# Messages and first convolution as one two by two by two block product in seven matmuls

## The chip, the core and the metric

The kernel runs on one core of a Trainium2 chip. The metric is the device time of one execution in microseconds (us); lower is better. The core has a matmul engine (TensorE, PE in the profile, with its weight loads as PEld), a vector engine (VectorE, DVE), an engine for activations and copies (ScalarE, ACT), a general one (GpSimd, POOL) and SyncE (SP), whose queue issues most DMAs. SBUF is the working memory, PSUM the banks that matmuls write and add into.

## What is computed

There are 64 graphs of 256 nodes with 256 features, all float32. Layer 0 is a normalised graph convolution with a residual; layer 1 is the large one. The parts that matter here:

```python
h = jnp.maximum(_layernorm(x, axis=-1), 0.0)          # x after layer 0
xc = jnp.transpose(h, (0, 2, 1))
c = relu(_bn(_conv1d(xc, conv1_w, 0), bn1_g, bn1_b, bn1_m, bn1_v))   # 1 tap: a matrix product
c = _bn(_conv1d(c, conv2_w, 8), ...)                  # 17 taps
x_conv = transpose(relu(c + xc))
s = h @ w_se.T + b_se                                 # 3 columns
sq = jnp.sum(s * s, axis=-1)
dist = sq[:, :, None] + sq[:, None, :] - 2.0 * einsum('bnd,bmd->bnm', s, s)
A = jnp.exp(-dist) * adj
msg = relu(h @ w_msg.T + b_msg)                       # messages
x_nmp = einsum('bnm,bmd->bnd', A, msg)
# a GRU cell with input [x_conv, x_nmp] and state h, then a residual
```

So each graph's h (256 x 256) is multiplied by w_msg (256 columns), by w_se (3 columns) and by the first convolution's scaled weights (256 columns). These are the products of this case.

## The kernel before

**Stages.** A first stage goes over the 64 graphs; a second one goes over them again for the gates of the GRU cell. The 17-tap convolution is done on four chunks of 16 graphs through a transform along the nodes: *spectra* (df), products per frequency (y) and an inverse made of adds on DVE and POOL. The first chunk's spectra, products and inverse, and before them the making of the transformed filters (fs), are "items" that are woven into the first stage.

**One turn of the first stage** (the loop over n, L1285 to L1361) works on several graphs at once. In order, on PE: `turn_h(n-2)` transposes h into hT (records ht); `aggregate(n)` and `project(n)` are layer 0's two products (ag, o); `turn_cols(n-4)`, for even n, transposes the small columns (st); `turn_adj(n+1)` transposes the next adjacency (at); `pass_messages(n-5)` multiplies A by the messages (nm); `messages(n-2)` is h times w_msg and w_se (ms); `distance(n-4)`, for even n, is the product for dist (di); `conv1(n-2)` is the first convolution (c). Between them stand calls of `item()`, eight a turn. While filters are made only the two calls `item(True)`, ahead of messages and ahead of conv1, take one.

**Order on the other engines.** All engines run their queues in the order in which the program issues. After each group of matmuls stands `beat(us)`. A beat does the work that has come due: `after(k, go)` puts `go` on the (k+1)th beat that follows, and what comes due on one beat runs in the order in which it was put there. Then `paced.issue` releases a share of the inverse's adds to DVE, POOL and ACT, by the us of the beat and an estimated cost of each operation. So a beat fixes an order, not a time.

**The work around the change.** After `project(n)`: the DVE rows (two of pre and two of x, `rows`, on the second beat, with the store x2d), their moments on the third, POOL's power and product (rs, nmr) on the fifth, ACT's two halves of h on the seventh and eighth. `turn_h` copies its bank to hT on its second beat, by ACT while paced work is left and else by DVE. `aggregate`, `turn_adj` and `pass_messages` copy their banks (aggT, adjT, xnT) with ACT on their second beat; POOL makes adjH from adjT one beat after that. The adjacency exponentials e are ACT's, the product aT is POOL's.

**Messages and conv1.** Each has a PSUM tile of its own (`ms` two banks, `c1` one; five banks of `ps` serve all else), which `own_bank` (L1014) fills with the bias by an ACT copy of 518 or 512 columns. `to_rows` (L1020) adds four matmuls onto it: two row blocks of 128 nodes times two halves of the features. In `messages`, DVE copies the three columns of w_se to `cols` and squares and sums them (`columns`), and ACT makes the messages with one Relu of 512 columns (mso); in `conv1` one ACT Relu of 512 columns makes c1o, which the store h1d takes. Both on the second beat after the matmuls; the next graph's bias copies on the third.

**Buffers.** Tiles of the pool `work` have two buffers unless another number is given: adjH, aggT, xnT and c1o have two, pre two.

Of the kernel before, what the change touches and what calls it, by code (L numbers as in the profile page):

```python
# [11 lines left out]
FP = mybir.dt.float32  # L12
# [173 lines left out]
def gnn_kernel(  # L186
# [11 lines left out]
    P = 128  # L198
# [48 lines left out]
    def after(beats, go):  # L247
        due.append([beats, go])
# [298 lines left out]
    with ExitStack() as one:  # L547
# [25 lines left out]
        nc.gpsimd.memset(mhalf, -0.5)  # L573

        w0T = wts.tile([P, DC, D], FP, tag="w0T", name="w0T")
        w1T = wts.tile([P, DC, D], FP, tag="w1T", name="w1T")

        wmT = wts.tile([P, DC, D + 3], FP, tag="wmT", name="wmT")
        b0B = wts.tile([P, D], FP, tag="b0B", name="b0B")
        b1B = wts.tile([P, 1, D], FP, tag="b1B", name="b1B")  # L580
        bmB = wts.tile([P, 1, D + 3], FP, tag="bmB", name="bmB")
        w2T = [
            taps.tile([P, KW, D], FP, tag=f"w2T{cc}", name=f"w2T_{cc}") for cc in range(DC)
        ]
# [116 lines left out]
        def small_loads():  # L701
            for k, v in enumerate((bn1_g, bn2_g, bn1_b, bn2_b, bn1_m, bn2_m, bn1_v, bn2_v)):
                sp.dma_start(
                    rows[DC * k : DC * (k + 1), :], v.rearrange("(c p) -> c p", p=P)
                )
            sp.dma_start(wsn, w_se)
            sp.dma_start(bmB[:, 0, 0:D], b_msg.partition_broadcast(P))
            sp.dma_start(bmB[:, 0, D : D + 3], b_se.partition_broadcast(P))

        def small_turns():  # L710

# [9 lines left out]
        def small_norms(t):  # L721

            vec.tensor_copy(bn, t[:, :16])
            ve = prep.tile([P, 4], FP, tag="ve", name="ve")
            vec.tensor_scalar(ve, bn[:, 12:16], EPS, None, ALU.add)
            for cc in range(DC):
                vec.tensor_copy(wmT[:, cc, D : D + 3], t[:, 16 + cc * 4 : 16 + cc * 4 + 3])
            rs = prep.tile([P, 4], FP, tag="rs", name="rs")
            pool.tensor_tensor(rs, ve, mhalf[:, :4], ALU.pow)

            def finish():
                vec.tensor_tensor(sc, bn[:, 0:4], rs, ALU.mult)
                ms = prep.tile([P, 4], FP, tag="ms", name="ms")
                vec.tensor_tensor(ms, bn[:, 8:12], sc, ALU.mult)
                vec.tensor_tensor(sh, bn[:, 4:8], ms, ALU.subtract)
                for c in range(DC):
                    vec.tensor_scalar(dg[:, c, :], ident, sh[:, c : c + 1], None, ALU.mult)
            after(2, finish)

        def small_shift():  # L740

            t = bank("t_b1")
            for c in range(DC):
                pe.matmul(t[:, c * P : (c + 1) * P], ones, dg[:, c, :], start=True, stop=True)

            def keep():
                vec.tensor_copy(b1B[:, 0, :], t[:, :D])
            after(0, keep)

        hold, nat = {}, {}  # L750

# [146 lines left out]
        def turn_adj(g, at=(1, 2), by=pool):  # L898
            s = st[g]
            t = bank(f"at_{g}").rearrange("p (c i) -> p c i", c=NB)  # L900
            for jc in range(NB):
                for ic in range(NB):
                    pe.transpose(
                        t[:, jc, ic * P : (ic + 1) * P], s["at"][:, ic, jc * P : (jc + 1) * P], ident
                    )

            def keep():
                s["adjT"] = work.tile([P, NB, N], FP, tag="adjT", name=f"adjT_{g}", bufs=6)
                act.copy(s["adjT"], t)

            def hat():
                s["adjH"] = work.tile([P, NB, N], FP, tag="adjH", name=f"adjH_{g}")
                by.tensor_tensor(s["adjH"], s["adjT"], eye, ALU.add)
            after(at[0], keep)
            if at[1] is None:
                return hat
            after(at[1], hat)

        def aggregate(g):
# [7 lines left out]
                    )  # L927

            def keep():
                s["aggT"] = work.tile([P, DC, N], FP, tag="aggT", name=f"aggT_{g}")  # L930
                act.copy(s["aggT"], t)
            after(1, keep)

        def project(g):
# [9 lines left out]
            def rows():  # L944
                s["x2"] = x2 = work.tile([P, NB, D], FP, tag="x2", name=f"x2_{g}")
                for ib in range(NB):
                    pre = small.tile([P, D], FP, tag="pre", name=f"pre_{g}_{ib}", bufs=2)
                    vec.scalar_tensor_tensor(
                        pre, t[:, ib, :], s["dis"][:, ib : ib + 1], b0B, ALU.mult, ALU.add
                    )  # L950
                    vec.scalar_tensor_tensor(
                        x2[:, ib, :], pre, 0.0, s["xt"][:, ib, :], ALU.max, ALU.add
                    )
# [39 lines left out]
        def turn_h(g, at=1, by=None):  # L993
# [10 lines left out]
            def keep():  # L1004
# [2 lines left out]
                (act.copy if by or any(paced.lines) else vec.tensor_copy)(s["hT"], t)  # L1007
                nc.sync.dma_start(hT_d[g].rearrange("p (c n) -> p c n", c=DC), s["hT"])
            after(at, keep)


        own = {}

        def own_bank(tag, k, bias):  # L1014
            width = bias.shape[2]
            shape = [P, NB, 512] if tag == "ms" else [P, NB, D]
            own[tag] = t = ps_own.tile(shape, FP, tag=tag, name=f"{tag}_{k}")
            act.copy(t[:, :, :width], bias.broadcast_to([P, NB, width]))

        def to_rows(g, tag, wT):  # L1020
            s, t = st[g], own.pop(tag)
            for nb in range(NB):
                for cc in range(DC):
                    pe.matmul(
                        t[:, nb, : wT.shape[2]], s["hT"][:, cc, nb * P : (nb + 1) * P],
                        wT[:, cc, :], start=False, stop=(cc == DC - 1), skip_group_check=True,
                    )
            return t

        def conv1(g):  # L1030
            t = to_rows(g, "c1", w1T)

            def keep():
                h1 = work.tile([P, NB, D], FP, tag="c1", name=f"c1o_{g}")
                act.activation(h1, t, AF.Relu)
                nc.sync.dma_start(h1_d[g].rearrange("p (c d) -> p c d", c=NB), h1)
            after(1, keep)
            if g + 1 < B:
                after(2, lambda: own_bank("c1", g + 1, b1B))

        def messages(g):

            s, t = st[g], to_rows(g, "ms", wmT)

            def columns():

                own = cols.rearrange("p b s (m k w) -> p b (s m) k w", m=2, k=2)[:, :, :, g % 2]
                vec.tensor_copy(
                    own[:, :, :, 0:3],
                    t[:, :, D : D + 3].unsqueeze(2).broadcast_to([P, NB, 4, 3]),  # L1050
                )
                s3 = own[:, :, 0, 0:3]
                sq = small.tile([P, NB, 3], FP, tag="sq", name=f"sq_{g}")
                vec.scalar_tensor_tensor(sq, s3, -0.5, s3, ALU.mult, ALU.mult)
# [2 lines left out]
                vec.tensor_reduce(own[:, :, 2:4, 3], twice, AX.X, ALU.add)  # L1057

            def keep():
                s["msg"] = work.tile([P, NB, D], FP, tag="ms", name=f"mso_{g}", bufs=4)  # L1060
                act.activation(s["msg"], t[:, :, :D], AF.Relu)
            after(1, columns)
            after(1, keep)
            if g + 1 < B:
                after(2, lambda: own_bank("ms", g + 1, bmB))

        def turn_cols(g):

# [43 lines left out]
        def pass_messages(g):  # L1112
# [7 lines left out]
                    )  # L1120

            def keep():
                xn = work.tile([P, DC, N], FP, tag="xnT", name=f"xnT_{g}")
                act.copy(xn, t)
                nc.sync.dma_start(xn_d[g].rearrange("p (c n) -> p c n", c=DC), xn)
                s.clear()
# [18 lines left out]
        act.activation(warm, mhalf[:, 0:1], AF.Relu)  # L1145

        full = eye.rearrange("p c d -> p (c d)")
        own_ms = ps_own.tile([P, NB, 512], FP, tag="ms", name="first_ms")
        own_c1 = ps_own.tile([P, NB, D], FP, tag="c1", name="first_c1")
        for r, t in enumerate((own_ms[:, 0, :], own_ms[:, 1, :], own_c1)):  # L1150
            at = slice(32 * r, 32 * (r + 1))
            pe.matmul(t, ident[at, :], full[at, :], start=True, stop=True)

        def stats(b):

# [9 lines left out]
        def begin():  # L1165
# [42 lines left out]
            aggregate(3)  # L1208
            beat(1.7)
            turn_adj(4)  # L1210
            own_bank("ms", 0, bmB)
            beat(0.4)
            project(2)
            beat(1.7)
# [1 line left out]
            small_shift()  # L1216
            beat(0.4)
            turn_part(w1T, nat_w1, 0, D, "w1", scale=sc[:, 0:DC])
            own_bank("c1", 0, b1B)
            load(3 * G)  # L1220
            project(3)
            beat(1.7)
            messages(0)
            beat(1.7)
            layer0_in(2 * G, range(2))
            conv1(0)
            beat(1.7)
            T(WI, 2)()
            L(WH, 0)()
            turn_h(1, 0, act)  # L1230
# [2 lines left out]
                go()  # L1233
            layer0_in(2 * G, range(2, NR))
            beat(0.4)
            messages(1)
            beat(1.7)
            later.pop(0)[1]()
            later[2].insert(0, T(WI, 4))
            conv1(1)  # L1240
            beat(1.7)
            weights_by[:] = []

        cv.bank, cv.beat = bank, beat
# [40 lines left out]
        for n in range(4, B + 5):  # L1285
# [27 lines left out]
                    after(4, lambda n=n: degrees(n + G))  # L1313
            beat(1.7)
            item()
            if even and n <= B + 2:
                turn_cols(n - 4)
            beat(0.2)
            if n + 1 < B:
                turn_adj(n + 1)  # L1320
            beat(0.4)
# [1 line left out]
            if n >= 5:  # L1323
                pass_messages(n - 5)
            beat(1.7)
            item(True)
            if n <= B + 1:
                messages(n - 2)
            beat(1.7)
            item()  # L1330
            if even and n <= B + 2:
# [4 lines left out]
                project(n)  # L1336
            beat(1.7)
            item(True)
            if n <= B:
                conv1(n - 2)  # L1340
            elif n == B + 2:
                conv1(B - 1)
            beat(1.7)
            item()
            if later:
                for go in later.pop(0):
# [331 lines left out]
```

## Time and profile before

| | |
|---|---|
| median of 3 runs | 2079.58 us (2076.08 to 2081.04) |
| span of the profiled execution | 2074.4 us |
| first stage in the span | until 844 us |
| of it: filters made (fs) | about 140 to 360 us |
| spectra (df) of the first chunk | about 362 to 478 us |
| products (y) of the first chunk | about 475 to 603 us |
| its inverse alone, no items | 603 to 844 us |
| granted TensorE clock, mean | 0.997 |

The profiled execution is one of the program; its span stands 5.2 us below the median of the runs. A record in a timeline has its start, its duration, engine, line, operation, what it writes and reads, and in brackets the idle time ahead of it and what ended that. Helpers issue most operations, so they all have one line (L102), and they are told apart by the names of their tiles. A float32 matmul stands in the records as two, which overlap, so start to start is the better measure of its cost. Groups that work on the two products, with the mean of a record:

| operation | records | mean |
|---|---|---|
| PE ms<-wmT,h2T, 259 columns | 512 | 391 ns |
| PE c<-w1T,h2T, 256 columns | 512 | 383 ns |
| ACT ms<-bmB, 518 columns (median) | 64 | 594 ns |
| ACT c<-b1B, 512 columns (median) | 64 | 590 ns |
| ACT mso<-ms, 512 columns (median) | 64 | 597 ns |
| ACT c1o<-c, 512 columns (median) | 64 | 597 ns |
| DVE cols<-ms, 24 columns (median) | 64 | 182 ns |

### The profile page before, as it was taken

What the parts mean: (1) busy time and instruction counts of PE and PEld (TensorE: products, weight loads), DVE (VectorE), ACT (ScalarE), POOL (GpSimd) and SP (SyncE); (2) the same over time, 40 slices, a digit from 0 to 9 for tenths busy, and PEclk for the clock granted to TensorE, in tenths of its full rate; (3) what the DMA queues carried; (4) which work ended last, traced back from release to release, by engine and by line L of the source; (5) the groups of instructions that cost most, each with busy time, mean ns of one, the idle gap of its engine ahead of it and who ended that gap; (6) DMA issues with size and microseconds to landing.
All of it is one profiled execution on the core that took longest, in us unless ns stands there. A gap on an engine that the chain in (4) does not pass through costs nothing. (4 is left out here: it accounts for less than half of the span.)

```text
span 2074.4 us, 31212 instructions
## 1 busy us (share of the span) xinstructions
PE 2029.9 (98%) x9977; PEld 1728.6 (83%) x9977; DVE 1403.6 (68%) x3172; ACT 999.2 (48%) x2171; POOL 1108.7 (53%) x1326
## 2 busy tenths in 40 slices
PE   7999999999999999999999999999999999999998
PEld 6877777888888787788888888888888888888887
DVE  5656666544688888237889815989924989965444
ACT  5756666665457676522344532234442234443333
POOL 4343333334775665347667527766626767644433
PEclk9999999999999999999999999999999999999999
DMA  8797987656765554656333455533446524322331
GB/s 282 261 259 245 265 257 248 208 178 224 240 206 198 178 178 138 212 178 204 122 117 117 137 176 190 168 101 118 124 152 199 155 92 129 116 87 89 95 96 61
DMA packets 292488, 352.84 MB, mean 170 GB/s; under 512 B 19523, under 2 KB 232150, under 8 KB 291670
## 3 DMA queue, kind: packets, MB, share of 16 engines
q1 hardware_dynamic: 292038, 346.40, 53.1%
q0 software_dynamic: 288, 4.46, 0.6%
q8 instruction: 80, 1.31, 0.3%
q14 instruction: 82, 0.67, 0.1%
HBM read 224.43 MB, written 126.35 MB: 169 GB/s over the span
## 5 line engine op out<-in xcount | busy, mean ns | idle before, releaser
L102 DVE TENSOR_TENSOR Xf<-y,k 128x256 f32<-128x256 f32 x184 | 69.0, 416 | 177.8 <-PE y L102 174.8
L102 DVE SCALAR_TENSOR_TENSOR Xf<-Xf 128x256 f32<-128x256 f32 (+1 forms) x248 | 185.1, 760 | 6.2 <-ACT Xf L102 5.1
L102 PE MATMUL ta<-T,S 128*128 128x256 f32 x768 | 186.6, 379 | 0.0
L102 PE MATMUL y<-wf,Xf 128*128 128x256 f32 x768 | 182.5, 380 | 1.8 <-DVE Xf L102 1.4
L102 POOL TENSOR_TENSOR rz<-u,p 128x256 f32<-128x256 f32 x64 | 47.8, 747 | 244.4 <-ACT u L102 244.4
L102 POOL TENSOR_TENSOR rs<-ve,mhalf 128x2 f32<-128x2 f32 x65 | 52.1, 801 | 220.0 <-DVE nm L102 218.7
L102 ACT ACTIVATE rz<-rz 128x512 f32<-128x512 f32 x128 | 80.3, 627 | 180.8 <-DVE rz L102 180.8
L102 PEld LDWEIGHTS y<-wf,Xf 128*128 128x128 f32 x768 | 143.9, 190 | 24.1 <-DVE Xf L102 2.6
L102 PEld LDWEIGHTS ta<-T,S 128*128 128x128 f32 x768 | 145.9, 190 | 19.8
L102 PE MATMUL n<-wiT,hx 128*128 128x256 f32 x512 | 152.3, 379 | 0.0
L102 POOL TENSOR_TENSOR xs<-Xf 128x256 f32<-128x256 f32 x92 | 69.8, 765 | 136.2 <-PE y L102 72.2
L102 DVE SCALAR_TENSOR_TENSOR h2l<-rz,h2l 128x256 f32<-128x256 f32 x128 | 102.9, 804 | 53.4 <-POOL h2l L102 53.4
L102 POOL TENSOR_TENSOR aT<-e,adjT 128x512 f32<-128x512 f32 x62 | 83.1, 1357 | 95.0 <-ACT e L102 95.0
L102 PE MATMUL ms<-wmT,h2T 128*128 128x259 f32 x512 | 127.2, 391 | 4.4 <-ACT h2T L102 4.4
L102 PE MATMUL n<-whT,hx 128*128 128x256 f32 x512 | 131.4, 379 | 0.0
L102 PE MATMUL n<-wiT,xcT 128*128 128x256 f32 x512 | 131.4, 379 | 0.0
L102 PE MATMUL nm<-aT,mso 128*128 128x256 f32 x512 | 123.3, 385 | 6.1 <-DVE pre L102 3.6
L102 PE MATMUL ag<-adjH,hs 128*128 128x256 f32 x512 | 124.3, 385 | 4.8 <-POOL adjH L102 2.7
L102 POOL TENSOR_TENSOR adjH<-adjT,eye 128x512 f32<-128x512 f32 x63 | 82.2, 1305 | 83.0 <-ACT adjT L102 81.2
L102 PE MATMUL o<-w0T,aggT 128*128 128x256 f32 x512 | 124.0, 385 | 1.4 <-ACT e L102 0.9
L102 PEld LDWEIGHTS ms<-wmT,h2T 128*128 128x128 f32 x512 | 97.8, 194 | 32.1 <-issue 12.9
L102 PE MATMUL c<-w1T,h2T 128*128 128x256 f32 x512 | 123.0, 383 | 0.0
(190 smaller groups left out, 5259.4 us busy)
## 6 DMA issues: line engine op xcount, KB each, us to landing
wf<-wfd SPq DMA_DIRECT2D x284, 256.0 KB
wfd<-fo SPq DMA_DIRECT2D x32, 576.0 KB
x2d<-x SPq DMA_DIRECT2D x64, 256.0 KB
h2d<-h SPq DMA_DIRECT2D x64, 256.0 KB
hTd<-h2T SPq DMA_DIRECT2D x64, 256.0 KB
h1d<-c1o SPq DMA_DIRECT2D x64, 256.0 KB
xnd<-xnT SPq DMA_DIRECT2D x64, 256.0 KB
h1l<-h1d SPq DMA_DIRECT2D x64, 256.0 KB
```

The costliest lines, as they stand in the source:

```text
L102: return self.tc.keep_in_program_order(getattr(self.engine, op)(*args, **kwargs))
```

## The change

hT of a graph is taken as a two by two block matrix (row blocks of nodes by halves of the features: a11, a21, a12, a22), and the weights as another: the columns of the messages with two of w_se (258 columns), beside those of the first convolution with the third of w_se and one column of zeros (258). The product of the two is made with seven block products in place of eight. For that

- four sums of hT's blocks (128 x 128) are made per graph, S0 and S1 by DVE, S3 and S2 by POOL (`h_inputs`, on the beat after hT's copy), and four sums of the weight blocks once (`h_weights`, on POOL);
- the seven matmuls go in two parts: `h_first` (four) where `messages` stood, `h_second` (three) where `conv1` stood. They use three banks, ta, tb and tc, of 258 columns. Three are partial sums that are read and then added to further: ACT copies p1, p5, u2 and p4 to SBUF (258 columns each), and DVE's four adds make the two halves of messages and of the convolution from a copy and a bank each;
- the two bias copies have 258 columns, and the second bias is the difference of the two; Relu is done in place in SBUF, on 512 columns each as before;
- w_se's columns come from two tiles, so DVE copies to `cols` twice, and this happens at the end of a turn, after `h_second`;
- `turn_cols` moves from ahead of `turn_adj` to behind `pass_messages`;
- adjH, aggT, xnT, c1o and pre have one buffer in place of two; the store h1d takes its rows from a tile of 258 columns a row block;
- the last graph's second part comes one turn earlier than its conv1 did, and the beat after `h_second` is 1.3 where that after `conv1` was 1.7.

```diff
@@ constants
-        w1T = wts.tile([P, DC, D], FP, tag="w1T", name="w1T")
-        wmT = wts.tile([P, DC, D + 3], FP, tag="wmT", name="wmT")
+        HC = D + 2
+        wh1 = wts.tile([P, 2, DC, HC], FP, tag="wh1", name="wh1")
+        wmT, w1T = wh1[:, 0], wh1[:, 1]
+        tw = wts.tile([P, 4, HC], FP, tag="tw", name="tw")
...
+        def h_weights():
+            b11, b21, b12, b22 = (wh1[:, w, c] for w in range(2) for c in range(DC))
+            sub(pool, tw[:, 0], b12, b11)
+            sub(pool, tw[:, 1], b22, tw[:, 0])
+            sub(pool, tw[:, 3], b21, tw[:, 1])
+            sub(pool, tw[:, 2], b22, b12)
@@ turn_h
             after(at, keep)
+            after(at + 1, lambda: h_inputs(g))
@@
+        def own_bank(tag, k):
+            own[tag] = t = ps_own.tile([P, HC], FP, tag=tag, name=f"{tag}_{k}")
+            act.copy(t, bmB if tag == "ha" else bdB)
+
+        def h_inputs(g):
+            s, hT = st[g], st[g]["hT"]
+            a11, a21, a12, a22 = (
+                hT[:, c, nb * P : (nb + 1) * P] for c in range(DC) for nb in range(NB)
+            )
+            S = [work.tile([P, P], FP, tag=f"hs{k}", name=f"hs{k}_{g}", bufs=1) for k in range(4)]
+            s["A"] = a11, a21, a12, a22
+            s["S"] = S
+            add(vec, S[0], a21, a22)
+            sub(vec, S[1], S[0], a11)
+            sub(pool, S[3], a12, S[1])
+            sub(pool, S[2], a11, a21)
+
+        def one(bank, a, b, start=False):
+            pe.matmul(bank, a, b, start=start, stop=True, skip_group_check=True)
+
+        def part_copied(s, g, key, tag, bank):
+            s[key] = t = work.tile([P, HC], FP, tag=tag, name=f"{key}_{g}", bufs=1)
+            act.copy(t, bank)
+
+        def h_first(g):
+            s = st[g]
+            a11, a21, a12, a22 = s["A"]
+            s["ta"], s["tc"] = ta, tc1 = own.pop("ha"), own.pop("hc")
+            tb = ps_own.tile([P, HC], FP, tag="hb", name=f"hb_{g}_0")
+            one(ta, a11, wmT[:, 0])
+            one(tb, a12, wmT[:, 1], True)
+            part_copied(s, g, "p1", "p1", ta)
+            one(tc1, s["S"][0], tw[:, 0])
+            one(ta, s["S"][1], tw[:, 1])
+
+            def c11():
+                s["msg"] = work.tile([P, NB, HC], FP, tag="ms", name=f"mso_{g}", bufs=4)
+                add(vec, s["msg"][:, 0], s["p1"], tb)
+            after(0, c11)
+            after(0, lambda: part_copied(s, g, "p5", "p5", tc1))
+            after(0, lambda: part_copied(s, g, "u2", "u2", ta))
+
+        def h_second(g):
+            s = st[g]
+            a11, a21, a12, a22 = s["A"]
+            ta, tc1 = s["ta"], s["tc"]
+            tb = ps_own.tile([P, HC], FP, tag="hb", name=f"hb_{g}_1")
+            one(tc1, s["S"][3], w1T[:, 1])
+            one(tb, a22, tw[:, 3], True)
+            s["h1"] = work.tile([P, NB, HC], FP, tag="c1", name=f"c1o_{g}", bufs=1)
+            part_copied(s, g, "p4", "p1", tb)
+            one(ta, s["S"][2], tw[:, 2])
+
+            def rows():
+                add(vec, s["h1"][:, 0], s["u2"], tc1)
+                add(vec, s["msg"][:, 1], s["p4"], ta)
+                add(vec, s["h1"][:, 1], s["p5"], ta)
+                if g + 1 < B:
+                    own_bank("hc", g + 1)
+                    own_bank("ha", g + 1)
+
+            def columns():
+                own = cols.rearrange("p b s (m k w) -> p b (s m) k w", m=2, k=2)[:, :, :, g % 2]
+                for of, at, n in ((s["msg"], 0, 2), (s["h1"], 2, 1)):
+                    vec.tensor_copy(
+                        own[:, :, :, at : at + n],
+                        of[:, :, D : D + n].unsqueeze(2).broadcast_to([P, NB, 4, n]),
+                    )
...
             def keep():
-                s["msg"] = work.tile([P, NB, D], FP, tag="ms", name=f"mso_{g}", bufs=4)
-                act.activation(s["msg"], t[:, :, :D], AF.Relu)
-            after(1, columns)
-            after(1, keep)
+                for t in (s["msg"], s["h1"]):
+                    act.activation(t[:, :, :D], t[:, :, :D], AF.Relu)
+                nc.sync.dma_start(h1_d[g].rearrange("p (c d) -> p c d", c=NB), s["h1"][:, :, :D])
+            after(0, rows)
+            after(0, columns)
+            after(0, keep)
@@ the loop
             beat(1.7)
             item()
-            if even and n <= B + 2:
-                turn_cols(n - 4)
-            beat(0.2)
             if n + 1 < B:
                 turn_adj(n + 1)
...
             beat(1.7)
+            if even and n <= B + 2:
+                turn_cols(n - 4)
+            beat(0.2)
             item(True)
             if n <= B + 1:
-                messages(n - 2)
+                h_first(n - 2)
             beat(1.7)
...
             item(True)
-            if n <= B:
-                conv1(n - 2)
-            elif n == B + 2:
-                conv1(B - 1)
-            beat(1.7)
+            if n <= B + 1:
+                h_second(n - 2)
+            beat(1.3)
```

## The prediction

> **What bounds the kernel now.** I read the page first, then busy time by stretches, then each engine's instructions in order of time for one turn of two stages, then the waits. In the page TensorE (PE) fills the span:
>
> ```profile
> span 2074.4 us, 31212 instructions
> ...
> PE 2029.9 (98%) x9977; PEld 1728.6 (83%) x9977; DVE 1403.6 (68%) x3172; ACT 999.2 (48%) x2171; POOL 1108.7 (53%) x1326
> ...
> L102 PE MATMUL ms<-wmT,h2T 128*128 128x259 f32 x512 | 127.2, 391 | 4.4 <-ACT h2T L102 4.4
> ```
>
> So a matmul less is time less, if nothing new makes PE wait. The averages hide the stages that are changed, which end at 844 us. By stretches (us; then busy PE, PEld, DVE, ACT, POOL): the filter products (156 to 350) and the stage's end, where no convolution product fills PE any more (603 to 818):
>
> ```profile
> 156.00:350.00 194.00, 194.00 (x1046) 138.35 (x1046) 133.75 (x378) 134.01 (x269) 68.42 (x91) 1.00 0.82 253
> ...
> 603.00:818.00 215.00, 206.97 (x1082) 174.12 (x1081) 185.26 (x510) 147.79 (x319) 128.59 (x143) 1.00 0.52 174
> ```
>
> In the second VectorE (DVE) is at 86%. One turn of it on PE, from the timeline:
>
> ```profile
> 657.98 1.89 PE L102 MATMUL nm<-aT,mso 128*128 128x256 f32 x8
> 659.71 1.91 PE L102 MATMUL ms<-wmT,h2T 128*128 128x259 f32 x8
> 661.46 1.89 PE L102 MATMUL o<-w0T,aggT 128*128 128x256 f32 x8
> 663.18 1.89 PE L102 MATMUL c<-w1T,h2T 128*128 128x256 f32 x8
> 664.91 0.60 PE L102 MATMUL ht<-ident,h 128*128 128x128 f32 x4
> ```
>
> Two records are one matmul. Start to start, four take 1.72 to 1.75 us (ms, o, c), so one costs 0.44; in the filter stretch ms takes 1.95 and c 1.83, so 0.46 to 0.49. The other engines in the same turn:
>
> ```profile
> 653.85 0.48 DVE L102 SCALAR_TENSOR_TENSOR pre<-o,dis,b0B 128x256 f32<-128x256 f32 x1 [0.95 <-PE o L102]
> ...
> 658.51 0.16 DVE L102 TENSOR_SCALAR nm<-mv 128x2 f32<-128x2 f32 x1
> ```
>
> and on POOL and ACT
>
> ```profile
> 658.68 1.15 POOL L102 TENSOR_TENSOR rs<-ve,mhalf 128x2 f32<-128x2 f32 x1 [2.25 <-DVE nm L102]
> ```
> ```profile
> 660.13 0.60 ACT L102 ACTIVATE h<-x,nmr,rs 128x256 f32<-128x256 f32 x1 [1.81 <-DMA hTd<-h2T]
> 660.64 0.56 ACT L102 COPY adjT<-at 128x512 f32<-128x512 f32 x1
> 661.10 0.60 ACT L102 ACTIVATE h<-x,nmr,rs 128x256 f32<-128x256 f32 x1
> 661.61 0.57 ACT L102 COPY xnT<-nm 128x512 f32<-128x512 f32 x1
> ```
>
> Read together: the projection o ends at 653.65, DVE's rows and moments of it end at 658.67, POOL's power and product at 660.09, and only then ScalarE (ACT) goes on, because its h is next in its queue. So ACT evicts nm at 661.61, 1.9 us after PE has begun ms. That lag is free today: nothing in ms waits for ACT.
>
> **The change, part by part.** *Removed:* four matmuls of 259 columns and four of 256 become seven of 258, one less per graph: 64 x 0.45 = 29 us of PE at most.
>
> *ACT.* Before, per graph: two bias copies and two Relu of 512 to 518 columns (0.594, 0.590, 0.597, 0.597 us). After: two bias copies and p1, p5, u2, p4 of 258 (nearest rows: ta<-brzB 377 ns, p<-ta and u<-ta 372 ns) and the same two Relu: 3.4 against 2.4 us, +1.06. The Trainium skill, "Perfetto Trace Analysis", Optimizing Scalar/DVE Operations, speaks against such splitting: each ScalarE operation has a fixed share, some 51 ns on PSUM, and larger operations are better. By that page four more operations and 518 more columns at 0.85 ns (590 less 372 ns over 256) give +0.64 us (an estimate); our rows, two sizes apart, say +1.06.
>
> *DVE.* Added per graph: four adds with one operand in PSUM (rz<-p,tb, 408 ns, 0.34 start to start), S0 and S1 of 128x128 (S<-hx, 281 ns, 0.2 start to start) and a second small copy to cols (182 ns): 4 x 0.34 + 0.4 + 0.15 + about 0.2 for results awaited in the queue = 2.1 us. Bounds: 1.8 and, where S0 and S1 meet POOL (S<-hx has a longest of 820 ns), 3.2. The row that shows such meetings is x<-pre,x, 427 ns median and 1130 at nine tenths.
> The Trainium skill, "SBUF — State Buffer", Who interferes with whom, says that a VectorE operation with two SBUF inputs is shut out for the whole of a GpSimd operation that reads SBUF. At POOL's 60% in the end stretch it would put S0 and S1 behind half a POOL operation each, some 0.8 us more per graph (my estimate) and 3 us by the sum; I stay with 2.1, since most S<-hx rows show no delay.
>
> *POOL.* S3 and S2 (S<-hx,S 458 ns), 0.9 us per graph, needed one half turn later: hidden behind o and di, 0.9 if not.
>
> *New waits.* The fourth matmul of the first half writes bank ta again, so it waits for ACT's copy p1, and everything on PE queues behind it: di, the projection, the second half. p1 stands in ACT's queue behind h and xnT of the turn (and L and R behind it). In the second half ACT's two bias copies, emitted with DVE's adds, wait for these, and hT, aggT, adjT, h, xnT queue behind them; the adds and cols stand on DVE before the moments (behind them where a filter item adds a beat).
>
> *End stretch, from the projection's end at 0.* Even graph projected: DVE rows start 0.2, last 2.0 (1.7 undisturbed, 2.8 in the turn shown), adds 1.0, cols 0.85, paced work 0.6, moments 1.44: 6.1. POOL to h 1.3: 7.4. ACT h 0.5, xnT 0.5, p1 0.5: 8.9. PE has done second half 1.4, ht 0.44, ag 1.73, at 0.44, nm 1.73 and three matmuls 1.35 by 7.1 and waits 1.8. Turn: 9.0 + 0.45 + o 1.73 = 11.2 for 9.53. Odd graph: rows to nmr ended 5.1 after the projection (642.84 to 647.91); with 1.85 more and ACT's three, p1 is done at 8.5 to 9.0 (four hs in ACT's queue) against 7.55, and with di the turn is 11.4 to 11.9 for 10.81. A pair takes 2.2 to 2.7 us longer; ten pairs: **+24**. Lower bound: DVE alone, 185.3 + 20 x 2.1 = 227 in a stretch of 215, +12. Upper, by 3.2 us: +45.
>
> *Filter stretch.* Even projected: rows 2.5 (x slowed), filter copies 1.2, moments 1.34, adds 1.0, cols 0.85 end at 7.0; ACT: two Relu 1.0, aggT, h, adjT, h, xnT 2.5, filter copies 1.0, p1 0.4: 11.9. PE is there after fs 1.24, 1.4, 0.44, 1.73, 0.44, 1.82, fs 1.15, 1.4 = 9.6. Turn 12.0 + 0.45 + 1.73 = 14.2 for 12.33. Odd: rows 0.8 shorter, L and R 0.5, st 0.44: late 1.55, less 0.45. A pair takes 3.0 longer, or 2.0 if the Relu needn't wait for cols (today's mso does: 16.9 us in 15 waits in this stretch). I take 2.75, eight pairs: **+22** (bounds -7 and +26).
>
> *The rest.* Spectrum turns (graphs 27 to 34): three spectra of 0.82 lie between projection and p1, ACT late some 0.9, less 0.45: +4 (-4, +8). Product turns (35 to 41): 7.8 us of products lie there and cover it: -3. Graphs 3 to 10: like the end stretch without paced work, +0.5 each: +4 (-4, +10). Start: four weight differences on POOL (T<-wiT,T 726 ns) end about 3 us after w1T, the second needed 2.5 after it; S0 after the hT that ms already waited 4.4 us for; turnover: 0.4 us shorter beats leave some 4 us of paced DVE work to the drain: +3 (0, +8). Moved: turn_cols, 0.44 of PE, goes behind nm and has no DMA; L and R then end about when di starts, counted above. The convolution's Relu comes a beat earlier and its h1d with it, still between x2d and hTd on SP's queue; graph 63 has its second half a turn earlier: nothing taken. One buffer for adjH, aggT, pre, xnT, h1: reuse comes a turn (9.5 us) later; free, if a DMA of h1 or xn lands in that; 1 KB pieces for h1 instead of 2: no cost taken.
>
> Sum: 24 + 22 + 4 - 3 + 4 + 3 = +54 on the span of 2074.4, 2128; the median of the runs, 2079.6, stands 5.2 above, so **2134**.
>
> **The rivals.**
> *A, the copies are in time.* If ACT reaches p1 before PE, the 29 us stand, less 3 at the start: 2053. For: PE is never kept by ACT longer than 4.4 us at a time today, and the gate stage has the same copies with PE at 99%. Against: the lag of 1.9 us just shown.
> *B, only DVE's sum decides.* The end stretch loses 12, the other 44 graphs gain 20, start 3: 2075, up to 2095 with some waits. For: 86% plus 20% of a turn is over 100%. Against: ACT's queue in the filter stretch.
> *C, single buffers.* DVE's first add waits until the h1 written a turn ago has landed, and all of DVE behind it. The trace has one such wait with two buffers: 6.8 us (c1o for h1d). It decides when landing takes over 9 us; at 1 us per graph on top of the sum, 2198. For: SP's queue held x2d back 106.7 us in 29 waits. Against: that one wait is alone.
>
> **How the numbers follow.** Forecast 0.61 (its own range 2095 to 2158), A 0.13, B 0.19, C 0.07. No change, within 0.3% (about what this kernel's runs can tell), is 2073 to 2086. Faster: A and some of B, 0.17; same 0.08; slower 0.75. The range 2070 to 2160 leaves out A and C, 0.20.
>
> **What would show it.** PE matmul `ta` waiting for ACT `p1`, 50 us or more in all, mostly before 350 and after 603; turns of 11 to 12 us in the end stretch and 14 to 15 in the filter one; DVE near 95% in the end stretch; ACT's bias copies waiting for DVE. It is wrong if the turns are shorter by 0.45 (A), if PE waits in the end stretch only, for DVE (B), or if DVE's add waits for a DMA (C).

## The result and the profile after

The changed kernel takes 2214.5 us (median of 4 runs, 2212.4 to 2215.7) beside 2077.9 for the kernel before on the same chip: ratio 1.0659, interval 1.0644 to 1.0674. The forecast was slower, by 54 us; it is slower by some 137. The page after, its head and the engines' sums:

```profile
span 2213.8 us, 32188 instructions
...
PE 2087.7 (94%) x9847; PEld 1728.2 (78%) x9847; DVE 1518.1 (69%) x3623; ACT 1048.3 (47%) x2427; POOL 1161.7 (52%) x1460
```

PE has 130 records fewer and is busy 58 us longer: more than the saving went into standing (short stands count as busy here) and into products at half speed. The other engines' sums are near what was worked out, a little under it: DVE +114.5 us, 1.8 a graph (forecast 64 x 2.1 = 134), ACT +49, 0.77 a graph (68, 1.06), POOL +53 (58). S0 and S1 took 0.29 us in the median (longest 1.34), so most met no delay, as assumed. What the prediction cites on larger operations is said there of a saturated engine; ACT is busy for 47% of the span here. Busy time by stretches (us; then PE, PEld, DVE, ACT, POOL, the granted clock, the DMA share, GB/s):

```profile
60.00:183.00 123.00, 95.18 (x481) 78.81 (x482) 71.72 (x230) 70.49 (x156) 42.22 (x62) 0.89 0.75 214
196.00:437.00 241.00, 241.00 (x1077) 155.20 (x1076) 169.17 (x518) 152.82 (x347) 84.60 (x127) 0.95 0.70 214
...
681.00:947.00 266.00, 220.06 (x1044) 170.38 (x1043) 218.85 (x649) 164.58 (x400) 144.35 (x186) 0.96 0.41 141
```

The clock was 1.00 in the like stretches before (58 to 139.5, 156 to 362 and 603 to 817 us). From the start of the transposes `ht` of one graph to those of another the stages took (us):

| stage | before | after | more | forecast |
|---|---|---|---|---|
| to the first `ht` | 29.3 | 36.8 | 7.5 | start and turnover: 3 |
| graphs 0 to 10 | 126.9 | 158.8 | 31.9 | 4 (for 3 to 10) |
| filter, 11 to 26 | 206.0 | 241.7 | 35.7 | 22 |
| spectra and products, 27 to 41 | 240.9 | 244.2 | 3.3 | 1 |
| end stretch, 42 to 61 | 214.5 | 265.1 | 50.6 | 24 |
| the rest | 1256.8 | 1267.2 | 10.4 | in the 3 |

What PE waited for (us in all, times, longest):

```profile
PE ha L102 <- ACT p L102: 35.9, 29, 3.7
PE ha L102 <- ACT h2T L102: 18.3, 18, 3.7
PE ha L102 <- DVE h2T L102: 16.0, 3, 14.0
PE di L102 <- ACT R L102: 5.0, 14, 0.7
PE hc L102 <- DVE hs L102: 4.0, 6, 2.6
```

The first is the wait of the forecast, the fourth product for the copy of P1, and 25.3 us of it lie in the end stretch. One of its turns, on PE and on ACT:

```profile
753.35 0.70 PE L102 MATMUL ha<-wh,h2T 128*128 128x258 f32 x2 [0.85 <-ACT h2T L102]
753.89 0.60 PE L102 MATMUL hb<-wh,h2T 128*128 128x258 f32 x2
754.33 0.60 PE L102 MATMUL hc<-tw,hs 128*128 128x258 f32 x2
756.65 0.70 PE L102 MATMUL ha<-tw,hs 128*128 128x258 f32 x2 [1.73 <-ACT p L102]
```
```profile
750.71 0.38 ACT L102 COPY hc<-bdB 128x258 f32<-128x258 f32 x1 [2.00 <-DVE c1o L102]
...
752.74 0.56 ACT L102 COPY h2T<-ht 128x512 f32<-128x512 f32 x1
...
755.25 0.60 ACT L102 ACTIVATE h<-x,nmr,rs 128x256 f32<-128x256 f32 x1 [0.98 <-POOL nmr L102]
755.76 0.56 ACT L102 COPY xnT<-nm 128x512 f32<-128x512 f32 x1
756.23 0.38 ACT L102 COPY p<-ha 128x258 f32<-128x258 f32 x1
```

ACT stands for DVE's adds (750.71) and again for POOL's nmr (755.25), and P1's copy stands behind both, as forecast. The copy of hT is behind the first too: `ht` ends at 748.6, its copy begins at 752.74, and P1's own product waits for it; that wait was not in the forecast.

In the filter stretch the list of PE's waits is empty, though its turns are 15.09 (even graphs) and 15.48 us (odd) where they were 13.6 and 12.33. The loss hides in the length of a group, and it shows in the list of the weight loads, PEld, for the filter products `fs` (196 to 437 us; before, in 156 to 362, waits of `fs` for ACT sum to 5.8 us):

```profile
PEld fs L102 <- ACT adjT L102: 12.4, 16, 0.8
PEld fs L102 <- ACT xnT L102: 6.2, 8, 0.8
PEld fs L102 <- ACT aggT L102: 3.9, 8, 0.5
PEld fs L102 <- DVE h2T L102: 3.4, 8, 0.5
```

One odd turn on PE, and ACT in it:

```profile
288.28 1.89 PE L102 MATMUL nm<-aT,mso 128*128 128x256 f32 x8
290.10 3.34 PE L102 MATMUL fs<-tp,tab 17*72 17x512 f32 x8
293.37 0.73 PE L102 MATMUL ha<-wh,h2T 128*128 128x258 f32 x2
293.91 1.06 PE L102 MATMUL hb<-wh,h2T 128*128 128x258 f32 x2
294.76 1.07 PE L102 MATMUL hc<-tw,hs 128*128 128x258 f32 x2
```
```profile
288.75 0.38 ACT L102 COPY hc<-bdB 128x258 f32<-128x258 f32 x1 [2.93 <-DVE c1o L102]
...
290.78 0.56 ACT L102 COPY aggT<-ag 128x512 f32<-128x512 f32 x1
291.24 0.60 ACT L102 ACTIVATE h<-x,nmr,rs 128x256 f32<-128x256 f32 x1
291.75 0.57 ACT L102 COPY adjT<-at 128x512 f32<-128x512 f32 x1
```

Four filter products `fs` take 3.34 us; the like group of this turn before took 1.44 (`fs` at 238.43; in even turns it is 3.3 for 1.22). Their starts are 290.10, 290.71, 291.39 and 292.37; DVE's copy of `ht` ends at 290.66, ACT's of `ag` at 291.34 and of `at` at 292.31. The last three products each start some 0.05 us after one of these: PE waits for one of its five turning PSUM banks each time. Ahead of ACT's copies stand its 2.93 us for DVE's adds, two Relu and a norm; which of them costs most is for the runs below. P1's copy ends at 294.58, before the fourth product (295.62) needs it.

Two more things show. At 171 us one stop of 14 us, on three engines:

```profile
171.24 0.42 DVE L102 TENSOR_TENSOR c1o<-u,hc 128x258 f32<-128x258 f32 x1 [13.81 <-DMA h1d<-c1o]
```
```profile
171.70 0.38 ACT L102 COPY hc<-bdB 128x258 f32<-128x258 f32 x1 [14.38 <-DVE c1o L102]
```
```profile
175.10 1.20 PE L102 MATMUL ha<-wh,h2T 128*128 128x258 f32 x2 [13.99 <-DVE h2T L102]
```

This is rival C's mechanism: the add waits for the store of the h1 made for the graph before, which had been issued at 158.35, behind ten loads of `tp` (146 to 154 us). And from 293.91 on the products take 0.86 us start to start, twice the usual 0.44. In the end stretch, with each product's usual start-to-start time taken from the distance to the next (an estimate, good to some 3 us), what is left over sums as follows: waits some 17 us before and 65 to 68 after, products at half speed none and 9 to 11, PE's own work 197 and 188. So the seven products save some 9 us there (20 x 0.44), as reckoned, against 59 lost. Over graphs 0 to 61 the half-speed excess is some 32 us after and 4 to 6 before.

In graphs 0 to 10 one more turn stands out, 20.9 us for 11.6. ACT scales the filter's weights (w2n) there in one go, its copies of `ag`, `nm` and P1 stand behind that, and PE's fourth product stands 3.68 us for P1:

```profile
72.08 4.46 ACT L102 ACTIVATE w2n<-w2n,sc 128x1088 f32<-128x1088 f32 x4
...
78.85 0.37 ACT L102 COPY p<-ha 128x258 f32<-128x258 f32 x1
```
```profile
79.28 1.23 PE L102 MATMUL ha<-tw,hs 128*128 128x258 f32 x2 [3.68 <-ACT p L102]
```

### The profile page after: what moved, and what is told of

The parts are those of the page before. It is cut to its first block, busy times and chain, and to the rows that moved or that the text cites. A ratio compares the mean times of both kernels' runs of the same rounds, so it can differ in the third digit from the quotient of the medians.

```text
span 2213.8 us, 32188 instructions
## 1 busy us (share of the span) xinstructions
PE 2087.7 (94%) x9847; PEld 1728.2 (78%) x9847; DVE 1518.1 (69%) x3623; ACT 1048.3 (47%) x2427; POOL 1161.7 (52%) x1460
## 5 line engine op out<-in xcount | busy, mean ns | idle before, releaser
L102 DVE SCALAR_TENSOR_TENSOR Xf<-Xf 128x256 f32<-128x256 f32 (+1 forms) x248 | 180.5, 742 | 4.4 <-ACT Xf L102 3.3
L102 DVE SCALAR_TENSOR_TENSOR pre<-o,dis,b0B 128x256 f32<-128x256 f32 x128 | 61.7, 482 | 116.3 <-PE o L102 114.0
L102 PE MATMUL o<-w0T,aggT 128*128 128x256 f32 x512 | 137.6, 416 | 0.9 <-ACT e L102 0.9
L102 PE MATMUL ag<-adjH,hs 128*128 128x256 f32 x512 | 129.7, 399 | 3.9 <-ACT wh L102 3.5
L102 PEld LDWEIGHTS o<-w0T,aggT 128*128 128x128 f32 x512 | 105.6, 211 | 28.0 <-issue 6.6
L102 PE MATMUL ha<-tw,hs 128*128 128x258 f32 x256 | 87.7, 427 | 36.6 <-ACT p L102 35.9
L102 ACT COPY k<-y 128x512 f32<-128x512 f32 x92 | 53.8, 585 | 128.1 <-PE y L102 110.8
```

Source lines behind the costliest of these rows:

```text
L102: return self.tc.keep_in_program_order(getattr(self.engine, op)(*args, **kwargs))
```

## The experiments

Each was run beside the kernel before on the same chip; "after" is the changed kernel. On these chips the kernel before took 2074.8 to 2078.4 us, so a difference of two rows' medians is good to some 4 us; the ratios are free of that. The stages' lengths (us) of all of them:

| run | median | ratio, interval | to first ht | 0-10 | filter | 27-41 | end | rest |
|---|---|---|---|---|---|---|---|---|
| after | 2214.5 | 1.0659 (1.0644, 1.0674) | 36.8 | 158.8 | 241.7 | 244.2 | 265.1 | 1267.2 |
| e1 h1 twice | 2211.3 | 1.0657 (1.0626, 1.0688) | 37.1 | 153.0 | 249.1 | 243.8 | 257.5 | 1269.1 |
| e2 before, single | 2109.5 | 1.0166 (1.0137, 1.0196) | 38.4 | 138.3 | 214.7 | 241.2 | 214.4 | 1258.8 |
| e3 norms late | 2177.9 | 1.0496 (1.0465, 1.0526) | 34.4 | 156.2 | 221.9 | 244.1 | 252.4 | 1267.3 |
| e4 bias, Relu late | 2221.9 | 1.0708 (1.0677, 1.0739) | 36.5 | 165.9 | 242.0 | 243.3 | 265.3 | 1269.5 |
| e5 before, DVE more | 2116.4 | 1.0182 (1.0153, 1.0212) | 29.2 | 136.2 | 213.1 | 242.6 | 232.4 | 1261.3 |
| e7 no P1 wait | 2193.7 | 1.0554 (1.0524, 1.0585) | 38.6 | 150.3 | 244.2 | 237.0 | 253.0 | 1268.6 |
| e8 room | 2199.0 | 1.0580 (1.0549, 1.0611) | 35.6 | 146.4 | 243.5 | 243.8 | 257.4 | 1271.4 |
| e9 room, norms late | 2158.7 | 1.0386 (1.0356, 1.0416) | 35.3 | 143.9 | 218.3 | 243.6 | 251.3 | 1265.8 |
| e10 S2 apart | 2162.9 | 1.0407 (1.0376, 1.0439) | 34.4 | 146.5 | 220.5 | 243.3 | 250.5 | 1266.0 |
| e11 bias, Relu late | 2159.2 | 1.0390 (1.0357, 1.0422) | 37.2 | 138.4 | 219.6 | 245.5 | 250.3 | 1267.1 |
| e12 no sums | 2135.7 | 1.0276 (1.0245, 1.0308) | 35.6 | 136.9 | 216.7 | 240.1 | 236.0 | 1269.0 |
| e13 statistics late | 2163.5 | 1.0419 (1.0389, 1.0449) | 37.4 | 142.5 | 214.7 | 248.1 | 255.1 | 1265.5 |
| e14 idle filled | 2203.2 | 1.0610 (1.0579, 1.0641) | 34.4 | 158.7 | 231.6 | 244.1 | 265.0 | 1267.9 |
| e15 no sums, no wait | 2127.9 | 1.0255 (1.0195, 1.0314) | 35.1 | 139.7 | 215.6 | 235.4 | 231.3 | 1266.8 |

**Single buffers.**

```
after:   "c1o" bufs=1 -> 2, pre written into x2, S2 in S0's buffer and made a beat later
before:  adjH, aggT, pre, xnT, c1o: bufs=1
```

> The changed kernel with two buffers for h1 (room for it: pre is made in place in x2, S2 takes the tile of S0 one beat later). Theory S (single buffer of h1 makes DVE wait for the store): the three waits of DVE for the store, 19.2 us in the changed kernel's trace, go, and what they slowed with them: 2185 to 2197. Theory Q (ACT's queue is late at p1, everything else follows): the same turns of 15.1 and 15.5 us in the filter stretch and 12 us in the end stretch, so not under 2185. If S were the whole, 2085.

> The kernel before with one buffer each for adjH, aggT, pre, xnT and h1, nothing else. S: DVE is not the engine that writes h1 here (ACT is), the one long landing near the start of the filter stretch is met all the same: 14 us or more, 2090 to 2115. Q: at most the few us of the first turns, 2078 to 2085.

h1 with two buffers gained almost nothing. The stop moved to the next single buffer: ACT's xnT waits 11.4 us for its own store, and PE's fourth product 11.7 for the P1 copy behind it. On the kernel before, the same single buffers alone cost some 34 us: 9 at the start, 14 in turn 9 (as after the change; turn 10 gives 4.5 back), 7 and 2 in turns 16 and 20, and none in the end stretch, whose length stays at 214.4. Its stop in turn 9, on ACT and PE:

```profile
157.23 0.60 ACT L102 ACTIVATE c1o<-c 128x512 f32<-128x512 f32 x1 [17.98 <-DMA h1d<-c1o]
```
```profile
159.02 3.78 PE L102 MATMUL o<-w0T,aggT 128*128 128x256 f32 x8 [12.07 <-ACT aggT L102]
```

So a store does land later than a turn, in the one place where ten small loads stand ahead of it on the queue, and C is real there; that these loads are the reason was not tested. In turns 16 and 20 no engine waits for a store; in turn 16 PE's products run at half speed from 250 to 258 us.

**The order on ScalarE.**

```
e3:  after(6, norm(0)); after(7, norm(1))  ->  after(8, ..); after(9, ..)   (from graph 4 on)
e4:  own_bank("hc"), own_bank("ha") out of rows into after(4, banks); after(0, keep) -> after(4, keep)
```

> The changed kernel with ACT's two halves of h two beats later from graph 4 on, so that p1 no longer stands behind an operation that waits for POOL. Q: in the end stretch p1 comes some 1.5 us earlier in each second turn and 0.5 in the others (20 us), in the filter stretch 0.5 to 1 (8 to 16 us): 2175 to 2190. Theory D (DVE's sum of work is the bound of the end stretch): nothing there, 2205 to 2215.

> The changed kernel with ACT's two bias copies and two Relu issued four beats later, behind the copies of hT, aggT, adjT and xnT, so that ACT's queue no longer stops for DVE's adds. Q: 2.5 to 3 us of lateness go in the filter stretch and 1 to 2 in the end stretch, 16 x 2.5 + 20 x 1 = 60 us with the clock that follows: 2135 to 2165. D: the end stretch stays at 12 us a turn, the filter stretch gains: 2175. S: unchanged or worse, since the store of h1 is issued later.

Two activations moved by two beats bring back 37 us (34 by the ratios), 20 of them in the filter stretch, where ACT's copies of `ag`, `at` and `nm` no longer have a norm between them, so that the banks come free sooner: odd graphs' turns fall from 15.48 to 12.74. Some 12 of the 20 are the clock, which is 1.00 over this stretch (0.95 after). The even turns stay at 15.1. Moving the copies that wait for DVE instead gains nothing: they then stand with the Relu in front of P1's copy (PE still waits 33.7 us for it), and the late store stops DVE for longer (28.2 us for 19.2). Nor is all of that a wait: in the end stretch the 13.2 us for hT's copy are gone and 9.2 for S0 (1.1 after) have come, but the granted clock there is 0.91 (0.96 after). So ACT's stand for the adds is not shown to be what the filter stretch lost by; the norm between the copies is.

**VectorE's sum.**

```
h1 = work.tile(...)
+ for k in range(6): vec.bn_stats(junk[:, 6*k:6*k+6], st[g]["hT"][:, 0, :])
```

> The kernel before with six more reads of 256 columns on VectorE in each graph's turn (about 0.34 us each by the trace, so 2.05 us a turn, close to what the change adds to VectorE with its adds; their results are used by nothing). Theory B, that VectorE's sum sets the end stretch (rival B): its 20 turns of 9.5 and 10.8 us grow by 1.3 us or more each and the span passes 2110. Theory Q, that what stands in line before what on ScalarE's and PE's queues sets the turns and not VectorE's sum: 2078 to 2095, as VectorE has 1.9 to 2.5 us free in these turns.

Theory Q fell here, and B held by its time but not by its turns: +38 us, of which 9 in graphs 0 to 10 and 18 in the end stretch, 0.9 a turn where B said 1.3 or more in each. DVE is busy 219.9 of 232 us there:

```profile
621.00:853.00 232.00, 212.82 (x1076) 176.42 (x1075) 219.87 (x620) 146.91 (x316) 123.55 (x143) 0.98 0.48 159
```

The growth isn't in every turn: six of the ten odd ones stay near 9.6 us or under, and of the even ones, which have the statistics of a pair, most grow by 0.8 to 1.6 us. The filter stretch grew by 7 in the same way.

**The P1 wait, and room for more buffers.**

```
e7:  one(ta, S1, tw[:, 1])  ->  one(tc1[:, 258:512], S1, tw[:, 1, :254], True)
e8:  e1's edits; xnT, aggT two buffers; aT written into e
e9:  e8 and e3's edit
```

> The changed kernel with its fourth product written to the spare columns of the hc bank (254 of its 258 columns), so that no product waits for ScalarE's copy of P1; U2 is then P1 alone, so the sum P1 + P6 is left out. Theory Q (the p1 wait is the largest of the path's new waits, 36 us of PE's waits in the changed kernel, and it costs the same again in the clock that falls after it): 2150 to 2180. Rival T (taking one wait away only moves the stand still to the next reader in line, ScalarE's copies of h2T and h): over 2195.

> The changed kernel with two buffers again for h1, xnT and aggT (room made by writing pre into x2, aT into e, S2 into S0's buffer and ones into an S buffer), nothing else moved. Theory S (single buffers whose store lands late cost the turns 3 to 9 and 16 about 35 us, and with xnT open as well no reader is left to take the stall over): 2165 to 2185, the stand still of 14 us near 160 us gone. Rival (the clogged landings stop PE through another tile, as after h1 alone): over 2200.

> The kernel of the run before it (two buffers for h1, xnT and aggT) with the two norm activations moved two beats later as in e3_norm_late. If the two causes are separate, their gains add: 2211 less about 35 less about 36, 2130 to 2150. If they share a cause (one queue that is late for either reason), under half of the second gain is left: 2155 to 2175.

In e7 (and e15) the product into the spare columns also takes, as far as can be told, what hc held out of the sum. Without the P1 wait the end stretch is 12 us shorter and 27-41 is 7; the filter stretch is not shorter, so the wait that the forecast put there isn't what holds it. 21 us in all, between the two theories but within 2 us of T's, and T's mechanism shows: in the end stretch PE's wait for R before `di` grows from 3.3 to 14.7 us. With room for h1, xnT and aggT the stop at 160 us is gone, but 15 us is all that is gained, not 30 or more: graph 10 gives 8 back, and the filter stretch's clock falls to 0.92. Norms late and room together give 56, some 4 more than the 37 and 15 added. In e9 an edit of this run put a new reader in line:

```profile
716.36 1.18 PE L102 MATMUL ha<-tw,hs 128*128 128x258 f32 x2 [2.31 <-POOL hs L102]
```

S2, made later to share a buffer, comes late from POOL, 19.0 us in the end stretch.

**What is left.**

```
e10: e9 with S2 in its own buffer, made with S3; aggT single
e11: e10, after(3, banks), after(7, keep)
e12: e10, S = a21, a22, a11, a12 (no sums)
```

> The kernel of e9 with S2 in a buffer of its own again, made in the turn's early part (room from aggT, single again). In e9 PE waited 19.0 us in the end stretch for S2, which GpSimd made late there, and some 5 us more went in the low clock after it. If that wait was e9's own, 2130 to 2145; if the stand still moves on to the next reader in line, over 2150.

> As e10, with ScalarE's bias copies three beats later (behind the copies of h2T, aggT and adjT) and its two Relu copies seven beats later (behind p5 and u2). Theory Q (in e9 and e10 the copies that wait for VectorE's adds still hold up h2T, aggT and adjT, and with the norms out of the way they no longer land in front of a late norm as in e4): 10 to 25 us below e10. Rival, as e4 showed: they stand in front of p1 instead, and the time is e10's or longer.

> As e10 without the four sums of blocks of hT (S0 and S1 on VectorE, S2 and S3 on GpSimd): the products take the blocks themselves, so the sums are left out. It prices the chain that stands between hT's copy and the third, fourth, fifth and seventh product, and 0.6 us of VectorE a graph. If VectorE's sum still sets the end stretch (e5: 2 us a graph cost 38): 10 to 20 us below e10. If ScalarE's and PE's order does: within 5 us of e10.

e10 missed: S2's wait went and the end stretch stayed at 250.5; PE now waits there for hT's copy (11.0 us), for h (10.4), for the first add (6.7) and P1 (3.2). So the stand does move on. e11 missed too, within the interval of e10; its odd filter turns are the shortest of all (11.76 us, 12.33 before), and its even ones 15 to 16.6. e12 says where the rest lies: without the four sums of blocks (0.6 us of DVE and 0.9 of POOL a graph) the time falls by 27 us, 14.5 of it in the end stretch, more than DVE's share of the sums (20 x 0.6). They stand between hT's copy and four of the seven products, and the granted clock of that stretch is 1.00 without them (0.98 in e10).

```
e13: row_moments after(1), after(2) -> after(5), after(6); degrees after(4) -> after(8)
e14: before the first fs of a turn: 4 x one(hc[:, 258:], ident, tw[:, 0, :254], True)
e15: e12 and e7's edit
```

> As e11, with VectorE's row moments and degrees of the pair two graphs on moved behind the even turn's projection (four or five beats later); nothing is added or left out. In e11 the even filter turns (14.96 us, odd 11.76) have VectorE in one unbroken line: rows, two fo copies, moments, the three adds, the copy of hT, S0 and S1, these statistics, and only then the fo copies whose banks the distance products wait for. Theory V (what is left is VectorE's line, by place as much as by sum): the filter stretch falls from 219.6 to 203 to 212 us, and the time by 8 to 20 us below e11. Rival W (ScalarE's copies, held by the adds, are what holds the banks): within 4 us of e11.

> The changed kernel with four products whose result is not used (into spare columns of the hc bank) put in front of the first filter products of each turn, where PE stands some 2 us for banks that ScalarE has not yet copied out. They take 1.75 us, less than the stand. Theory C (PE's half speed phases, about 14 us in this stretch, come from its standing still there): the filter stretch falls from 241.7 to 227 to 234 us, with no half speed phase in it. Rival D (the low clock has another cause, or the products add their time): 240 us or longer.

> As e12 (two buffers for h1 and xnT, norms late, no sums of blocks of hT) and in addition the fourth product in spare columns as in e7, so that nothing waits for the copy of P1; the operand sums and P1 + P6 are left out. What is left of the change is then the three wide adds and one add of VectorE, ScalarE's copies and the order of issue. If the parts found so far are separate (P1 wait 20 alone, of which e12 still shows half): 2110 to 2128, the end stretch 222 to 230 us instead of 236. If the stand moves on to the next late reader once more: 2130 or longer.

e13 is neither theory's: the even filter turns fall from 14.96 to 13.97 us, but the stretch as a whole by 5, and the end stretch and the early turns give it back, with PE waiting for S0 (34.5 us in all). This order doesn't mend DVE's line; what is late only changes its name. e15 stands at the upper edge of its range, but its gain over e12, 5 to 8 us, is not clear of its interval (1.0195 to 1.0314). 53 us remain (2127.9 against 2075.0 on that chip) with neither operand sums nor P1 wait. In one even turn of its end stretch DVE is busy 11.01 of 11.46 us (the even turns of the kernel before were at 86 to 97%):

```profile
693.69:705.15 11.46, 10.65 (x59) 8.49 (x58) 11.01 (x34) 9.76 (x24) 5.05 (x5) 1.00 0.70 227
```

e14 adds work and is faster. Its four products share the bank in which h1 is summed and, as far as can be told, leave the preset bias bdB out of it; the instructions and their order are otherwise those of the changed kernel. An even turn of it on PE:

```profile
299.99 1.88 PE L102 MATMUL hc<-tw,ident 128*128 128x254 f32 x8
301.80 1.59 PE L102 MATMUL fs<-tp,tab 17*72 17x512 f32 x8
303.32 0.70 PE L102 MATMUL ha<-wh,h2T 128*128 128x258 f32 x2
```

The 1.81 us of products fit into the stand and `fs` ends as late in the turn as without them (8.1 us after its start, 7.7 in odd turns, in both kernels). All even turns but one keep their length, the odd ones fall from 15.48 to 13.80 us, since nothing in the stretch runs at half speed any more, and the filter stretch falls from 241.7 to 231.6; the other stages stay as they were, but for 2 us at the start.

No version beat the kernel before; the best that leave nothing out, e9 and e11, are 3.9% slower (interval 3.6 to 4.2).

## Why the forecast was right in direction and wrong in size

The direction does not prove the sum. The forecast gave 46 of its 54 us to the wait for P1, and without that wait the kernel is still 5.5% slower (e7). Three terms failed: the cause in the filter stretch (PSUM banks, not P1), the step "one buffer: free", and the size of the end stretch.

- **PE saves 0.44 us a graph, 29 in all.** Right: some 9 us in the end stretch's 20 turns.
- **The P1 wait in the end stretch, +24.** The mechanism was right, line by line, and the size was not: +50.6. The step's upper bound, +45, did not hold it either. It put one lateness on the path, DVE and POOL to ACT's h to P1. In the trace the same stand of ACT makes the copy of hT late as well (13.2 us of PE's waits in this stretch), S0 and S1 come after that, and 9 to 11 us went into products at half speed, a term that the sum didn't have. I had priced DVE's sum as a lower bound (+12) and not as a cost of its own beside the waits; on the kernel before, 2 us of DVE a graph cost 18 there. (The line read for ACT's h, at 660.13, names the DMA hTd, 0.04 us after POOL's end. That one line doesn't show POOL as the cause; the list of waits before the change does, with 39.4 us in 30 waits of h for POOL's nmr.)
- **The P1 wait in the filter stretch, +22.** This step failed in its cause. PE does not wait for P1 there (e7: no gain); it waits for PSUM banks, which ACT and DVE empty late. The sum followed ACT's queue to P1's copy well (done 11.3 us after the projection's end at 283.24, forecast 11.9) and didn't ask which banks the copies ahead of it hold, and who needs one sooner: the four `fs` products, directly behind nm. Had PE been there at 9.6 us, as forecast, it would have stood for P1; the stand for banks takes that one's place (argued from these times; no run took the bank stand alone away). Measured +35.7, of which some 12 is half speed. The sign that was named, 50 us or more of waits for P1, came to 35.9, none of it in this stretch.
- **Graphs 3 to 10, +4 (bounds -4, +10).** It was +32 for graphs 0 to 10. The step "one buffer: free, if a DMA lands within a turn" failed for some 12 of it: 12.4 come back with more buffers (e8), and single buffers cost the kernel before 11.4 there (e2), 14 us of it in turn 9 alone, 9.54 to 23.71. The one wait of 6.8 us that I saw with two buffers was the sign: it lay in this place, and I took it as alone. Another 9 lie in the turn in which ACT scales the filter weights, which the sum had left out; without the P1 wait it is 17.6 us in place of 20.9 (e7). The rest is not settled.
- **Start and turnover, +3.** +7.5 and +10.4. e2 shows the first (38.4 with the five single buffers on the kernel before, 29.3 without; the changed kernels lie between 34.4 and 38.6). In the second PE's waits up to 985 us are for hT's copy, S0, P1, R, the columns, aT and xnT, one behind the other, with products at half speed between; no run shortened it (e7 1268.6, e12 1269.0), so its parts are not settled.
- **Spectrum and product turns, +4 and -3.** +1.4 and +1.8: the cover by other products was there, less of the saving.
- **DVE near 95% in the end stretch.** 82% over the stretch, since the turns grew; 92 to 96% in eight of the ten even turns.
- **Rivals.** A fell. C was real, in two or three turns and the start, for 15 to 34 us of the loss, not per graph. B was half right: DVE's sum costs 38 on the kernel before, where I had let it cost nothing net.

The parts don't add up cleanly to 137, and they overlap. By their own runs: norms ahead of the copies 34 to 40, with the half speed of the filter stretch (10 to 12) in it; single buffers 15 (taken off) to 34 (put on); operand sums 27; P1 wait 21, or 5 to 8 on e12. What remains in e15, 53, is not explained in full: e5 pays 38 us for 112 us more of DVE, and e15 has 74 more than the kernel before, which at that rate is some 25 (an estimate). A run that takes the wide adds away was not made, so that share is argued, not shown, and the rest stays open.

## What to carry to other kernels

When a copy is added or made to wait on an in-order engine, follow everything behind it, the copies that free PSUM banks first: PE may stand for a bank long before it stands for the new value, and that can show as a long group of matmuls and among the waits of the weight loads, with nothing in PE's own list. Give back a second buffer only after looking for the latest landing of its store in the trace, near bursts of small loads above all, and not for the usual one. A matmul saved is worth less than its price if it hands two microseconds a turn to an engine that is already at 86% where the matmul runs.

## What the runs showed of the hardware

Short, repeated stands of PE cost twice. In the filter stretch no weight load of `fs` stood longer than 0.8 us, and the stands of one group add to some 2 us; yet once in two turns (30.7 us), after an odd turn's `fs`, the clock was halved for 3.4 us (products 0.86 us start to start for 0.43):

```profile
290.50:293.91 3.41, 3.41 (x10) 1.08 (x9) 2.03 (x5) 3.41 (x8) 2.38 (x3) 1.00 0.78 290
293.91:297.32 3.41, 3.41 (x9) 2.69 (x8) 0.42 (x1) 2.23 (x6) 1.91 (x5) 0.50 0.92 302
```

The granted clock over the stretch was 0.95; in e3, where a group takes 2.3 us, and with the stand filled by unused products it was 1.00:

```profile
193.00:424.50 231.50, 230.52 (x1210) 164.81 (x1209) 169.98 (x519) 151.63 (x349) 84.51 (x127) 1.00 0.74 222
```

The Trainium skill, "TensorE: Matmul & The Clock Gate", A second HAM failure mode: psum-queue depth-cycling, tells of PE pausing between groups as it turns through PSUM banks, often enough that its clock keeps switching between half and full. Rows and rule agree here, with float32 products and pauses inside a group, and e14 shows what the filling is worth, 10 us.

A store of 256 KB that follows ten loads of the filter's `tp` on the queue let the add that waited for it go some 13 us after its issue (158.35 to 171.24); of 64 turns only three show such a wait (19.2 us in all).
